# Last chunk of an attention and quantised feed-forward kernel: a tile's residual and butterflies issued ahead of a unit's division, its transposes ahead of the value products

## The chip, the cores and the metric

The kernel runs on one core of one Trainium2 chip. Such a core has five engines with a queue of instructions each: TensorE (PE in the profile; PEld is its loading of weights), VectorE (DVE), ScalarE (ACT), GpSimd (POOL) and SyncE (SP), which here only issues transfers. Each engine takes its own queue strictly in order and waits for others by semaphores. The metric is the time of one execution on the device, in microseconds (us); lower is better.

## The reference

The input x has 8 sequences of 1024 rows of 512 numbers. Cut to what matters:

```python
def attn(x, Wq, bq, Wk, bk, Wv, bv, Wo, bo):          # 16 heads of 32
    Q, K, V = (split_heads(x @ W.T + b) for W, b in ((Wq, bq), (Wk, bk), (Wv, bv)))
    scores = einsum('bhid,bhjd->bhij', Q, K) / sqrt(32)
    delta = t[:, None] - t[None, :]
    scores = where(delta < 0, -inf, scores) - delta   # causal, with a decay by distance
    out = einsum('bhij,bhjd->bhid', softmax(scores), V)
    return join_heads(out) @ Wo.T + bo

def ffn(x, weight):
    xh = x @ H                                        # Hadamard matrix, 512 x 512
    scale = clip(max(abs(xh), axis=-1), 1e-05) / 7
    xq = clip(round(xh / scale), -8, 7) * scale       # 4 bits
    return einsum('bsi,oi->bso', xq, ternary(weight))

x = x + layernorm(attn(layernorm(x), Wq, bq, Wk, bk, Wv, bv, Wo, bo))
x = x + layernorm(ffn(layernorm(x), weight))
```

## The kernel before

Rows are worked on in 16 chunks of 512, two to a sequence; a chunk has four tiles of 128 rows. Since the score falls by one for each row of distance, only a band of keys is used: a block of 128 queries sees its own 128 keys and the 128 before them. (A flag, `ok`, is worked out near the end from the largest products; if it says that the band isn't enough, a general path runs after it. With the inputs here it doesn't.)

**Units.** Attention is done in units: 256 queries (half a chunk) of four heads, so eight units to a chunk, in two halves of four. A unit has four steps. `scores()` puts 48 small products on TensorE (L571) into one PSUM tile `s`, and four exponentials on ScalarE (L585) from `s` into `pr`. `mask()` is one `affine_select` on GpSimd over `pr` (L596). `values()` multiplies `pr` with V (L626) and with ones, for the sums of the softmax (L637), into the PSUM tile `av`. `divide()` is four VectorE instructions (L655, L657, L659, L660) that read `av` and write a part of `oT`, the attention's output transposed. There is one buffer of `av` alone: the `values()` of a unit can start on TensorE only when the `divide()` of the unit before it has read `av` to its end (L660).

**Rests.** What follows attention is done tile by tile by a generator, `rest`; `steps(gen, n)` lets it run over n of its yields. Its steps: load the residual rows `xr` (L182); project with Wo into `o_ps` (L153); `y`, its statistics (L187, L126, L127 on VectorE) and one over the deviation, `rstd_a`, on GpSimd (L119, L120), then `ca` (L191); the residual sum `x1` (L194) and the two butterfly stages of the Hadamard transform, `u` (L198, L199) and `w` (L202, L203), on VectorE; four transposes of `w` into `wT_ps` (L210) and a copy of them to SBUF on ScalarE (L212); the product with the 128x128 Hadamard matrix into `h_ps` (L218) and its sum of squares (L226); the row's largest value `sc` (L238) and the scale (L240 to L243); the quantised row `qf` on ScalarE (L246) and `qi` on VectorE (L248); transposes of `qi` (L255) and their copy (L257); the product with the ternary weights into `f_ps` (L153 again, bf16); `y2` (L264); its statistics, and the last sum and the transfer out (L281 to L286). The last five tiles also have idle products put ahead of some of these, the warm products: L208 ahead of the transposes of `w`, L216 ahead of the Hadamard product, L253 ahead of the transposes of `qi`. Their results are overwritten.

**PSUM banks.** The rests share three banks, and `bank(held)`, `bank(one)`, `bank(two)` name the one that the next tile gets.

**The last chunk.** All order is written out by hand: each engine gets its instructions in the order in which the program issues them. In 15 of the 16 chunks the units are interleaved with the projections of the next chunk. The last chunk has no next one, and its loop (from `for u in range(2, 2 * NG, 2)`) interleaves units with rests alone: two units and one whole rest to a turn. In a turn, `late`, `rest_b` and `rest_a` are three tiles at different steps: `rest_a` is projected (`o_ps`, `y`) in one turn, becomes `rest_b` in the next, and there gets its transposes, its Hadamard product and all up to `y2`; then it is `late`. Before the loop comes a first turn written out by itself, and after it the tail, whose order is a string of letters.

There are four places where a tile's `x1`, butterflies and transposes meet two divisions; this text numbers them by turn. In place 1 the tile is 0_2 (tile 2 of the sequence's first chunk) and the units are 0 and 1 of the last chunk; in place 2 it is tile 0_3 with units 2 and 3; in place 3 tile 1_0 with units 4 and 5; in place 4 tile 1_1 with units 6 and 7, at the start of the tail. The first unit of each pair is called the even one, the second the odd one.

Of the kernel before, what the change touches and what calls it, by code (L numbers as in the profile page):

```python
# [40 lines left out]
def sandwich_kernel(  # L41
# [262 lines left out]
    def band():  # L304
# [212 lines left out]
        def diagonal(col, n):  # L517
            diag = row.tile([P, P], F32, tag="diag", name=f"diag_{n}", bufs=1)
            nc.vector.tensor_scalar(diag, ident, col, None, ALU.mult)
            return diag  # L520

        def spread_max(diag, n):

            ps = pools.ps_m.tile([P, P], F32, tag="pm", name=f"m_ps_{n}")
            nc.tensor.matmul(ps, ones, diag, start=True, stop=True)
            m = small.tile([P, 1], F32, tag="spread", name=f"spread_{n}")
            nc.vector.tensor_reduce(m, ps, AX.X, ALU.max)
            return m
# [263 lines left out]
        def steps(gen, count):  # L792
            for _ in range(count):
                if gen is not None:
                    next(gen)
# [15 lines left out]
        def bank(at):  # L811
            pools.ps_m.named = at
# [3 lines left out]
        held, one, two = 0, 1, 2  # L816
        unit = None
        rest_a = rest_b = None
        for at, ch in enumerate(chunks[:-1]):
# [7 lines left out]
            for u in range(0, 2 * NG, 2):  # L827

                new = Unit(ch, before, u)
# [6 lines left out]
                unit = new  # L836
# [13 lines left out]
                rest_b = rest_a  # L850
# [5 lines left out]
                rest_a = next(rests_due) if at or u >= 4 else None  # L856
# [9 lines left out]
                new = Unit(ch, before, u + 1)  # L866
                new.scores()
                unit.values()
                if u >= 4:
                    held, one, two = one, two, held  # L870
# [21 lines left out]
                unit = new  # L892
                if u == 6:
# [11 lines left out]
                    held, two = two, held  # L905
                else:
# [6 lines left out]
                    held, one, two = one, two, held  # L913
# [9 lines left out]
        new = Unit(ch, before, 0)  # L923
# [3 lines left out]
        unit = new  # L927
        steps(rest_a, 1)
        new = Unit(ch, before, 1)
        new.scores()  # L930
        unit.mask()
        rest_b, rest_a = rest_a, next(rests_due)
# [5 lines left out]
        steps(rest_b, 1)  # L938
        steps(rest_a, 1)
        unit.values()  # L940
        steps(rest_b, 1)
        new.mask()
        unit.divide()
        unit = new
        for u in range(2, 2 * NG, 2):
            late, rest_b, rest_a = rest_b, rest_a, next(rests_due)
            steps(rest_b, 1)
            new = Unit(ch, before, u)
            new.scores()
            unit.values()  # L950
            unit.divide()
            unit = new
            unit.mask()
            bank(held)
            steps(rest_b, 1)
            bank(one)
            steps(rest_b, 2)
            steps(late, 1)
            steps(rest_b, 1)
            new = Unit(ch, before, u + 1)  # L960
            new.scores()
            bank(two)
            steps(rest_a, 1)
            steps(rest_b, 1)
            new.mask()
            steps(late, 1)
            bank(held)
            steps(rest_b, 1)
            unit.values()
            steps(rest_a, 1)  # L970
            unit.divide()
            unit = new
            bank(one)
            steps(rest_b, 2)
            if u == 2:
                diag = diagonal(allmax, "all")
            elif u == 4:
                bank(held)
                okm = spread_max(diag, "all")
                nc.vector.tensor_scalar(ok, okm, (BAND_LIMIT / SLACK) ** 2, None, ALU.is_le)  # L980
            one, two = two, one

        late, rest_b, rest_a = rest_b, rest_a, next(rests_due)
        rest_c = next(rests_due)
        tails = {"l": late, "b": rest_b, "a": rest_a, "c": rest_c}
        steps(rest_b, 1)
        unit.values()
        unit.divide()
        order = "b0 b1 b l b a2 b l b0 a b1 c0 b a c a2 a1 b c a a c0 a c2 c c a0 a1 b c a c0 a c2 c c a c"
        for step in order.split():  # L990
            if step[1:]:
                bank((held, one, two)[int(step[1:])])
# [237 lines left out]
    with tc.manual_schedule():  # L1230
        band()
# [47 lines left out]
```

## Time and profile before

Three runs took 1395.66, 1396.66 and 1398.48 us; the median is 1396.66.

| what | value |
|---|---|
| the profiled execution's own time | 1396.07 us |
| its span, from the first to the last instruction | 1394.3 us |
| mean granted TensorE clock | 0.995 |
| first scores of the last chunk on TensorE | 1295.98 us |
| from there to the end | 98.3 us |
| TensorE busy, 1250 to 1290 us (loop of the other chunks) | 39.91 of 40 us |
| TensorE busy, 1310 to 1350 us (last chunk) | 36.29 of 40 us |
| VectorE busy, 1310 to 1350 us | 28.08 of 40 us |
| GpSimd busy, 1310 to 1350 us | 18.10 of 40 us |

A line of the timeline gives the start and the length of an instruction in us, its engine, its line in the kernel, its operation, the tile that it writes and those that it reads, and in brackets how long its engine was idle before it and whose end released it. A line of the stretches gives start and end, then the busy time of each engine in it with the number of its instructions, then the TensorE clock that was granted as a share of full speed, and the share and rate of the transfers. The page's chain of waits is empty for this run, so that the order of events has to be read from the timelines.

### The profile page before, as it was taken

To read this page: it belongs to the slowest core of one execution; us is meant where nothing else is said; L and a number is where in the kernel's file an instruction comes from. 1 tells how busy PE (TensorE), PEld (TensorE's weight loads), DVE (VectorE), ACT (ScalarE), POOL (GpSimd) and SP (SyncE) were. 2 spreads that over 40 slices of the span, in tenths; PEclk is the share of its full clock that TensorE was granted. 3 is DMA by queue.
4 is the path that set the end of the run, shared out by engine and by line. 5 is a ranking of instruction groups with operands and counts; after the bars stand their busy time and mean duration, and the time that the engine had idled before them with its cause. 6 is when DMAs were issued, how large, how long until landed. Compare 5 with 4: busy or idle time off the path is not lost.

```text
span 1394.3 us, 35003 instructions
## 1 busy us (share of the span) xinstructions
PE 1363.4 (98%) x14504; PEld 967.5 (69%) x14504; DVE 1015.7 (73%) x2167; ACT 681.2 (49%) x1176; POOL 892.0 (64%) x1280
## 2 busy tenths in 40 slices
PE   9999999999999999999999999999999999999895
PEld 5577777777767777767776777777776777766553
DVE  5467777777777776777777777877777777777675
ACT  3345454545445455554545545445544545535442
POOL 4565758576576767658676676757757666665434
PEclk9999999999999999999999999999999999999998
DMA  6010011011011011011011011011101101000010
GB/s 228 8 47 24 24 47 46 24 47 47 24 47 47 24 47 47 32 39 47 30 41 46 25 47 47 28 43 47 40 31 47 47 24 47 25 23 32 32 39 33
DMA packets 31750, 58.23 MB, mean 42 GB/s; under 512 B 4064, under 2 KB 4448, under 8 KB 31584
## 3 DMA queue, kind: packets, MB, share of 16 engines
q1 hardware_dynamic: 30720, 54.87, 11.4%
q8 instruction: 116, 1.90, 0.5%
q10 hardware_dynamic: 864, 1.05, 0.2%
q14 instruction: 50, 0.41, 0.1%
HBM read 39.13 MB, written 16.78 MB: 40 GB/s over the span
## 4 chain that ended last, share of the span: by engine, by line


## 5 line engine op out<-in xcount | busy, mean ns | idle before, releaser
L585 ACT ACTIVATE pr<-s,bias 128x512 f32<-128x512 f32 (+1 forms) x512 | 295.3, 660 | 138.5 <-PE s L571 138.5
L610 POOL TENSOR_TENSOR both<-pr 128x1024 f32<-128x1024 f32 (+1 forms) x120 | 250.5, 2088 | 5.2
L153 PE MATMUL o_ps<-wo_sb,oT 128*128 128x512 f32 x512 | 236.1, 604 | 0.6
L596 POOL TENSOR_SCALAR_AFFINE_SELECT pr<-pr 128x1024 f32<-128x1024 f32 x128 | 150.0, 1172 | 108.2 <-ACT pr L585 103.8
L153 PEld LDWEIGHTS o_ps<-wo_sb,oT 128*128 128x128 f32 x512 | 93.2, 192 | 95.2 <-issue 92.5
L187 DVE TENSOR_TENSOR y<-o_ps,bo 128x512 f32<-128x512 f32 x64 | 44.2, 691 | 150.5 <-PE o_ps L153 150.5
L626 PE MATMUL av<-pr,v 128*32 128x128 f32 (+1 forms) x2816 | 130.7, 316 | 1.8 <-DVE oT L660 1.8
L571 PE MATMUL s<-qT,kT 32*64 32x192 f32 (+2 forms) x5632 | 119.9, 285 | 1.5 <-ACT pr L585 1.5
L571 PEld LDWEIGHTS s<-qT,kT 32*64 32x64 f32 x5632 | 99.8, 131 | 31.0 <-issue 21.6
L141 ACT ACTIVATE xn<-xc,nmr,rstd_n 128x512 f32<-128x512 f32 x60 | 48.8, 814 | 140.0 <-POOL nmr L139 140.0
L119 POOL TENSOR_SCALAR rstd_a<-mv_a 128x1 f32<-128x1 f32 x64 | 13.9, 217 | 142.7 <-DVE mv_a L127 141.5
L226 ACT ACTIVATE wT<-h_ps 128x512 f32<-128x512 f32 x64 | 38.2, 597 | 133.8 <-PE h_ps L218 133.8
L626 PEld LDWEIGHTS av<-pr,v 128*32 128x32 f32 x2816 | 74.9, 110 | 35.4 <-issue 1.8
L212 ACT COPY wT<-wT_ps 128x512 f32<-128x512 f32 x64 | 37.5, 585 | 123.4 <-PE wT_ps L210 123.4
L238 DVE TENSOR_REDUCE sc<-h_ps 128x1 f32<-128x512 f32 x64 | 44.1, 689 | 63.8 <-ACT wT L226 63.8
L119 POOL TENSOR_SCALAR rstd_c<-mv_c 128x1 f32<-128x1 f32 x64 | 14.7, 229 | 116.1 <-DVE mv_c L127 116.0
L285 POOL TENSOR_TENSOR y<-y,x 128x512 f32<-128x512 f32 x63 | 80.6, 1279 | 1.3 <-ACT y L284 1.3
L637 PE MATMUL av<-both,ones 128*32 128x256 f32 x960 | 74.2, 381 | 0.5 <-POOL both L614 0.5
L218 PEld LDWEIGHTS h_ps<-had_sb,wT 128*128 128x128 f32 x512 | 66.8, 192 | 6.2 <-ACT wT L212 3.3
L218 PE MATMUL h_ps<-had_sb,wT 128*128 128x128 f32 x512 | 68.1, 276 | 2.1 <-ACT wT L212 2.1
L153 PE MATMUL f_ps<-ternT,qiT 128*128 128x512 bf16 x256 | 66.2, 382 | 2.4 <-ACT qiT L257 2.4
L146 ACT COPY xnT<-xnT_ps 128x512 f32<-128x512 f32 x60 | 35.2, 586 | 56.8 <-PE xnT_ps L145 56.8
(213 smaller groups left out, 3100.7 us busy)
## 6 DMA issues: line engine op xcount, KB each, us to landing
xr<-in_x SPq DMA_DIRECT2D x64, 256.0 KB, 2.9
out<-y SPq DMA_DIRECT2D x63, 256.0 KB, 2.0
xc<-in_x SPq DMA_DIRECT2D x60, 256.0 KB, 2.7
wv_sb<-in_wvT ACTq DMA_DIRECT2D x4, 256.0 KB, 5.1
x<-in_x SPq DMA_DIRECT2D x4, 256.0 KB, 4.9
wk_sb<-in_wkT SPq DMA_DIRECT2D x1, 1024.0 KB, 6.7
wq_sb<-in_wqT SPq DMA_DIRECT2D x1, 1024.0 KB, 9.0
wf_sb<-in_wf SPq DMA_DIRECT2D x1, 1024.0 KB, 10.7
```

The source lines that it names most:

```text
L141: nc.scalar.activation(xn, xc, AF.Identity, bias=nmr, scale=r)
L153: nc.tensor.matmul(ps, lhs(k), rhs(k), start=(k == 0), stop=(k == KD - 1))
L187: nc.vector.tensor_tensor(y, ps, bo2, ALU.add)
L218: nc.tensor.matmul(xh[:, k * P : (k + 1) * P], wT[:, k, :], had_sb if k else had0_sb, start=True, stop=True,)
L238: nc.vector.tensor_reduce(sc, xh, AX.X, ALU.max, apply_absolute_value=True)
L285: nc.gpsimd.tensor_tensor(y2, y2, x1, ALU.add)
L571: nc.tensor.matmul(s[half * hp : (half + 1) * hp, hh, column[which] + c0 : column[which] + c1], kc.kT[hsl, g, k0 : k0 + hp], ch.qT[hsl, g, ...
L585: nc.scalar.activation(pr[:, :, r0:, own, cols], s5[:, :, r0:, own, cols], AF.Exp, bias=ch.bias[:, own, h : h + 1],)
L596: nc.gpsimd.affine_select(out=own, in_=own, compare_op=ALU.is_ge, fill=0.0, base=0, pattern=[[0, HPG], [0, 2], [1, P]], channel_multiplier=-1,
L610: engine.tensor_tensor(self.both[:, :, r0:], pr[:, :, r0:, 0, :], pr[:, :, r0:, 1, :], ALU.add)
L626: nc.tensor.matmul(av[hh * HD : (hh + 1) * HD, 0, qc : qc + w], kc.v[:, at, h * HD : (h + 1) * HD], pr[:, hh, sc : sc + w], start=(at_part ...
L637: nc.tensor.matmul(av[hh * HD : (hh + 1) * HD, 1, :], ones[:, :HD], self.both[:, hh].rearrange("p r c -> p (r c)") if own is None else sel ...
```

## The change

Four things are moved in the last chunk, and nothing is added or taken away.

- In the first turn and in each turn of the loop the step that holds a tile's `x1` and butterflies (L194 to L203) is issued ahead of the division of the even unit, where it was issued behind it. In the first turn the `y2` of the tile before (L264) moves behind the division too.
- The step that holds the transposes of `w` with their warm products and the copy (L208, L210, L212) is issued ahead of the value products of the odd unit, where it was behind them and behind their division.
- The product that spreads the largest value for the flag (L525, in the turn u = 4) gets the bank `two` in place of `held`.
- At the tail the transposes are issued ahead of the value products of the last unit, and the string of the tail begins one step later.

On the queues this gives: TensorE has L208 and L210 of the four tiles ahead of the odd unit's L626 and L637; VectorE has L194 to L203 of the four tiles ahead of the even unit's L655 to L660; ScalarE and GpSimd have the same order as before; on SyncE the load of `xr` for tile 1_2 stands ahead of the read of the flag, where it stood behind it.

```diff
         steps(rest_b, 1)
         steps(rest_a, 1)
         unit.values()
+        new.mask()
+        steps(rest_a, 1)
+        unit.divide()
         steps(rest_b, 1)
-        new.mask()
-        unit.divide()
         unit = new
         for u in range(2, 2 * NG, 2):
             late, rest_b, rest_a = rest_b, rest_a, next(rests_due)
-            steps(rest_b, 1)
             new = Unit(ch, before, u)
             new.scores()
+            bank(held)
+            steps(rest_b, 1)
             unit.values()
             unit.divide()
             unit = new
             unit.mask()
-            bank(held)
-            steps(rest_b, 1)
             bank(one)
             steps(rest_b, 2)
...
             bank(held)
             steps(rest_b, 1)
             unit.values()
-            steps(rest_a, 1)
+            steps(rest_a, 2)
             unit.divide()
             unit = new
             bank(one)
...
             elif u == 4:
-                bank(held)
+                bank(two)
                 okm = spread_max(diag, "all")
...
         tails = {"l": late, "b": rest_b, "a": rest_a, "c": rest_c}
+        bank(held)
         steps(rest_b, 1)
         unit.values()
         unit.divide()
-        order = "b0 b1 b l b a2 b l b0 a b1 c0 b a c a2 a1 b c a a c0 a c2 c c a0 a1 b c a c0 a c2 c c a c"
+        order = "b1 b l b a2 b l b0 a b1 c0 b a c a2 a1 b c a a c0 a c2 c c a0 a1 b c a c0 a c2 c c a c"
```

## The prediction

> **What bounds the kernel now.** I read the busy shares first, then TensorE's waits between 1308 and 1362 us (the chain of waits is empty), then the last chunk's timelines, engine by engine.
>
> ```profile
> PE 1363.4 (98%) x14504; PEld 967.5 (69%) x14504; DVE 1015.7 (73%) x2167; ACT 681.2 (49%) x1176; POOL 892.0 (64%) x1280
> ```
>
> TensorE is nearly always busy, but the change touches only the last chunk, where it waits (total us, times, longest):
>
> ```profile
> PE qiT_ps L255 <- DVE qi L248: 2.3, 3, 0.8
> PE av L626 <- DVE oT L660: 1.8, 2, 0.9
> PE h_ps L218 <- ACT wT L212: 1.5, 4, 0.7
> ```
>
> The third wait is for the copy of the transposes, which the change puts beside the value products. The second is the odd unit's value products waiting for the even unit's division, and that division the change delays. Place 2, TensorE, then VectorE with GpSimd's `rstd_a`:
>
> ```profile
> 1324.55 0.99 PE L571 MATMUL s<-qT,kT 32*64 32x192 f32 x48
> 1325.49 1.08 PE L626 MATMUL av<-pr,v 128*32 128x256 f32 x24
> ...
> 1327.36 1.09 PE L208 MATMUL wT_ps<-ident 128*128 128x128 f32 x8
> 1328.29 0.76 PE L210 MATMUL wT_ps<-ident,w 128*128 128x128 f32 x4
> ...
> 1329.78 1.16 PE L218 MATMUL h_ps<-had_sb,wT 128*128 128x128 f32 x8 [0.28 <-ACT wT L212]
> ```
>
> ```profile
> 1322.69 0.18 DVE L127 BATCH_NORM_AGGREGATE mv_a<-st_a 128x2 f32<-128x6 f32 x1
> 1323.72 0.45 DVE L655 STREAM_TRANSPOSE sumT<-av 128x256 f32<-128x256 f32 x1 [0.85 <-PE av L637]
> ...
> 1324.92 0.42 DVE L660 TENSOR_TENSOR oT<-av,rn 128x256 f32<-128x256 f32 x1
> ...
> 1326.11 0.75 DVE L194 SCALAR_TENSOR_TENSOR x<-y,rstd_a,xr 128x512 f32<-128x512 f32 x1
> ...
> 1328.37 0.44 DVE L655 STREAM_TRANSPOSE sumT<-av 128x256 f32<-128x256 f32 x1
> ...
> 1323.27 0.57 POOL L120 TENSOR_TENSOR rstd_a<-rstd_a,neghalf 128x1 f32<-128x1 f32 x1
> ```
>
> The reader is to see that the even division ends at 1325.34, just ahead of the value products at 1325.49: it costs TensorE nothing here, with no room left. The whole place hangs on one loop: `qi` of a tile, `y` and statistics of the next, division, odd value products, Hadamard product `h_ps`, next `qi`.
>
> **The change part by part.** I time a place from the end of `qi` (Q) to the start of L218, and keep what follows L218 as it is: from there to the next Q it was 6.42 us at place 2 (1329.78 to 1336.21) as at place 1 (1314.90 to 1321.32), set by ScalarE's squares, the odd exponentials and `qf`, none of which change order.
>
> *Places 2 to 4, new sum.* Statistics end at Q+1.55 (1322.87 against Q = 1321.32), `rstd_a` at Q+2.52 (1323.84). `x1` now starts there, 0.03 later, Q+2.55 (that step after L120 is 0.03 at 1373.40 to 1373.43). From the start of `x1` to the start of the transposing L655 behind it are 2.26 (1326.11 to 1328.37): the division starts at Q+4.81, lasts 1.62 (1323.72 to 1325.34) and ends at Q+6.43. TensorE takes a released value product 0.15 later (oT ends 1355.32, L626 at 1355.47): Q+6.58. Value products and sums take 1.87 (1325.49 to 1327.36): Q+8.45. Two warm products L216 behind them, four records, take half of the eight L208 records' 0.93 (1327.36 to 1328.29), 0.46: L218 at Q+8.91. The transposes themselves cost nothing: scores end at Q+4.17, eight warm records fill to Q+5.10, `w` is ready near Q+5.03, they end by Q+5.7, the copy on ScalarE follows the even exponentials at Q+6.69 and ends at Q+7.3. The value products from Q+6.58 to Q+8.45 hide it; without that cover it would cost the old 0.28.
>
> L218 was at Q+8.46 in place 2, at Q+8.66 in place 3 (1336.21 to 1344.87; it holds L525, 0.31, which now falls into the wait) and at Q+8.30 in place 4 (1351.30 to 1359.60). So: **+0.45, +0.25, +0.61**. Bounds: 0.15 more each if the warm products take the 0.61 of their record; 0.6 less each (then -0.2 at place 2) if they vanish beside the wait (0.46) and `x1` with its butterflies takes its bare steps, 0.75 + 4 x 0.34 = 2.11 in place of 2.26. I take the middle, since TensorE showed that spacing of warm records and VectorE these 2.26 in place 3 too (1341.19 to 1343.45).
>
> *Place 1.* There GpSimd's mask of the odd unit (L596) stands right behind `rstd_a` and `ca`, where VectorE now begins `x1`. What then happens the loop of earlier chunks shows:
>
> ```profile
> 123.37 0.43 DVE L198 TENSOR_TENSOR u<-x 128x256 f32<-128x256 f32 x1
> 123.38 1.38 POOL L596 TENSOR_SCALAR_AFFINE_SELECT pr<-pr 128x1024 f32<-128x1024 f32 x1 [1.67 <-ACT pr L585]
> 123.71 1.33 DVE L199 TENSOR_TENSOR u<-x 128x256 f32<-128x256 f32 x1
> ```
>
> One butterfly takes 1.33 in place of 0.42: +0.91. `rstd_a` ends at 1309.59, `x1` starts at 1309.62, `ca` meets it (0.81, as at 1368.19) and ends about 1310.50, the mask then takes its turn behind L198 and holds L199. The division starts at 1309.62 + 2.26 + 0.91 = 1312.79, ends 1314.41; value products at 1314.56 where they were at 1311.52; 1.87 later, without warm products for this tile, L218 at 1316.43, where it was at 1314.90: **+1.53** (+0.62 if the mask slips by).
>
> *Tail.* `o_ps` of tile 1_2 waits for the last division: 0.13 behind the sums (1353.56 to 1353.69), 1.62, 0.15, so 1.90 after them, where L218's group ends 1.45 after them (0.46 + 0.99). These 0.45 fall into TensorE's wait of 0.54 before L255 at 1364.95: 0; with that cover gone, 0.45.
>
> *The rest of the diff.* The late `y2` of place 1 and L525 in bank `two`: L527 reads it about one us after the division, the next writer there is L216, two us after it: 0. The `xr` load ahead of the flag's read on SyncE is wanted a turn of 15 us later and lands in 2.9: 0. GpSimd and ScalarE keep their order; queued behind the waiting value products are L216, L218 and the odd scores, which is the loss already counted.
>
> *Clock.* Sum so far: 1.53 + 0.45 + 0.25 + 0.61 = **+2.84**. But place 1 now leaves TensorE nearly empty: from 1310.53 to about 1313.0 for `w`, about 0.6 of transposes, and until 1314.56 for the division, 3.4 of 4.0 us. The slow time of the trace lasts 3.41 us, so here are stretches of that length:
>
> ```profile
> 1298.35:1301.76 3.41, 1.45 (x57) 1.25 (x54) 2.67 (x8) 2.99 (x6) 2.20 (x2) 1.00 0.40 114
> 1301.76:1305.17 3.41, 3.41 (x6) 1.33 (x5) 0.00 (x0) 2.07 (x4) 0.00 (x0) 0.50 0.12 45
> ...
> 1363.20:1366.61 3.41, 1.91 (x13) 0.87 (x12) 2.28 (x6) 2.06 (x3) 2.21 (x5) 1.00 0.02 5
> 1366.61:1370.02 3.41, 3.41 (x11) 1.66 (x10) 2.56 (x5) 0.00 (x0) 2.13 (x4) 1.00 0.20 77
> ```
>
> After a stretch with TensorE busy 1.45 the clock (first number behind the counts) is 0.50 for one stretch, after 1.91 it stays 1.00. Place 1 will have a stretch busy for well under 1.7 wherever such stretches begin. A slow one costs at most 1.65: the eight `o_ps` records at 1301.60 took 5.35, at 1331.79 3.70. Part of it falls on the waiting itself; between 0 and 1.65 I take 1.2, nearer the row with full work, since value products, L218 and scores fill it.
>
> [...]
>
> Total **+4.04**. The profiled execution is 1394.3 of span and 1.8 around it, 1396.07, and 0.6 below the median: 1396.07 + 4.04 = **1400.1 us**.
>
> **The rivals.** *Stalls without the clock* (22 of 100): +2.84, or +1.93 without the clash with the mask: 1398.0 to 1398.9. For it: where the 3.41 us stretches begin differs from run to run. Against it: 3.4 of 4 us empty.
>
> *A stretch that no longer falls badly* (11): the run before lost 1.65 to the slow clock at 1301.76, before any moved instruction; if the new run begins its stretches elsewhere, +2.84 − 1.65 gives 1397.3. The 2.8 us between the three runs speak for such play.
>
> *Clock lost at place 4 as well* (10): pauses of about 0.8 and 1.0 there; +1.2 more, 1401.3.
>
> *The other side, faster* (7): the transposes fill the pauses and the division doesn't hold TensorE. Then the old pauses go: 0.92 + 0.87 for `oT`, 0.67 + 3 x 0.28 for the copy, 3.3 in all: 1392.8. It decides by one thing, whether the division ends before the transposes do (Q+5.7); by the rows it ends at Q+6.43, and only a `rstd_a` 0.7 us earlier, with GpSimd as it is, would turn it. That the change doesn't do what it says I don't expect: the queues show it.
>
> **How the numbers follow.** Forecast 50, the others 22, 11, 10, 7. The forecast's own range is 1398.9 (clock at 0) to 1401.5 (clock at 1.65, warm products at their longest, the tail's 0.45). With eight in ten wanted, I go down past the second and third cases to 1397.0 and up to 1402.4. A measurement of this kernel tells about 0.2%, 2.8 us. Over 1399.45: 0.46 of the forecast's 0.50, the place 4 case and 0.08 of the second, 0.64; below 1393.9 the last case, 0.07; within, the rest, 0.29.
>
> **What would show it.** Right: in places 2 to 4, L194 starting where L655 stood, a pause of about 0.9 before the odd L626 put down to oT, none before L218, Q to Q growing to 15.3 us; in place 1 a butterfly of 1.3 us, L626 3 us after the old distance from the scores' start, a slow stretch behind it. Wrong: L626 following L210 with no pause, turns shorter than 14.9 us, or a late L218 that the tail makes good.

## The result, and the profile after

| | before | changed |
|---|---|---|
| median (11 runs each) | 1397.08 us | 1400.77 us |
| lowest to highest | 1394.46 to 1398.77 | 1398.60 to 1402.78 |
| profiled execution, and its span | 1396.07, 1394.3 | 1402.69, 1401.0 |

The changed kernel takes 1.0026 times as long, with a 95% interval of 1.0017 to 1.0035: +3.6 us (2.4 to 4.9). The chain of waits is empty again. TensorE's waits between 1308 and 1366 us of the changed kernel (total us, times, longest):

```profile
PE av L626 <- DVE oT L660: 3.7, 4, 1.1
PE wT_ps L210 <- DVE w L202: 2.5, 2, 2.1
PE qiT_ps L255 <- DVE qi L248: 2.4, 3, 0.8
```

The wait for the copy of the transposes (1.5 us before) is gone. The wait of the odd value products for the even division has come at all four places, where it was at two, and at two places there is a wait for `w` that was not there. Place 2, TensorE's timeline, then VectorE's:

```profile
1327.82 0.99 PE L571 MATMUL s<-qT,kT 32*64 32x192 f32 x48
1328.74 1.09 PE L208 MATMUL wT_ps<-ident 128*128 128x128 f32 x8
1329.67 0.60 PE L210 MATMUL wT_ps<-ident,w 128*128 128x128 f32 x4
1331.16 1.08 PE L626 MATMUL av<-pr,v 128*32 128x256 f32 x24 [0.90 <-DVE oT L660]
1332.03 1.07 PE L637 MATMUL av<-pr,ones 128*32 128x256 f32 x16
1333.03 0.71 PE L216 MATMUL h_ps<-ones 128*128 128x128 f32 x4
1333.58 1.06 PE L218 MATMUL h_ps<-had_sb,wT 128*128 128x128 f32 x8
```

```profile
1323.47 1.12 DVE L248 TENSOR_SCALAR qi<-qf 128x512 bf16<-128x512 f32 x1 [1.28 <-ACT qf L246]
...
1327.14 0.75 DVE L194 SCALAR_TENSOR_TENSOR x<-y,rstd_a,xr 128x512 f32<-128x512 f32 x1 [1.00 <-POOL rstd_a L120]
...
1329.40 0.44 DVE L655 STREAM_TRANSPOSE sumT<-av 128x256 f32<-128x256 f32 x1
...
1330.59 0.42 DVE L660 TENSOR_TENSOR oT<-av,rn 128x256 f32<-128x256 f32 x1
```

`x1` now begins 1.00 us after VectorE fell idle, released by GpSimd. The division starts 2.26 behind it, and TensorE, done with its transposes, stands for 0.90 until the division's last instruction lets `av` go. Place 1, VectorE and then GpSimd:

```profile
1309.96 0.75 DVE L194 SCALAR_TENSOR_TENSOR x<-y,rstd_a,xr 128x512 f32<-128x512 f32 x1 [1.00 <-POOL rstd_a L120]
1310.75 0.42 DVE L198 TENSOR_TENSOR u<-x 128x256 f32<-128x256 f32 x1
1311.09 1.33 DVE L199 TENSOR_TENSOR u<-x 128x256 f32<-128x256 f32 x1
...
1310.80 1.34 POOL L596 TENSOR_SCALAR_AFFINE_SELECT pr<-pr 128x1024 f32<-128x1024 f32 x1
```

and what TensorE makes of it:

```profile
1313.03 0.79 PE L210 MATMUL wT_ps<-ident,w 128*128 128x128 f32 x4 [2.09 <-DVE w L202]
1314.89 1.93 PE L626 MATMUL av<-pr,v 128*32 128x256 f32 x24 [1.08 <-DVE oT L660]
1316.57 1.65 PE L637 MATMUL av<-pr,ones 128*32 128x256 f32 x16
```

The value products take 1.93 and 1.65 us in place of 1.08 and 1.07. The stretches say why (columns as before; the first number behind the last bracket is TensorE's clock):

```profile
1310.97:1314.39 3.42, 0.79 (x4) 0.45 (x4) 3.28 (x8) 2.96 (x5) 2.03 (x2) 1.00 0.25 79
1314.39:1317.80 3.41, 2.91 (x36) 1.98 (x40) 1.01 (x2) 0.05 (x1) 0.25 (x1) 0.50 0.02 5
1317.80:1321.21 3.41, 3.41 (x67) 2.39 (x60) 2.60 (x6) 1.55 (x4) 0.74 (x2) 1.00 0.00 0
1358.77:1362.18 3.41, 1.89 (x18) 1.19 (x20) 3.27 (x9) 0.59 (x1) 0.00 (x0) 1.00 0.24 77
1362.18:1365.59 3.41, 3.41 (x42) 2.15 (x32) 0.51 (x2) 0.00 (x0) 0.00 (x0) 0.50 0.01 2
```

Half clock follows place 1's empty stretch and, in this execution, place 4's too. The two profiled spans differ by 6.70 us, more than the medians. By distances between instructions this splits as follows. The last chunk's first scores come 2.03 later (1298.01 against 1295.98), through code that is the same. `o_ps` of the first turn takes 3.65 in place of 5.35: -1.70. From the even scores (place 1) or the end of `qi` (places 2 to 4) to the Hadamard product L218: +2.92, +0.53, +0.33, +2.33. From L218 to the next `qi`: -0.17 in all. From the last of these L218 to the end: +0.43. So the four places cost 5.9 us in this execution, 3.0 of it clock.

### The profile page after: what moved, and what is told of

Same layout as the page of the kernel before. It is cut to its first block, busy times and chain, and to the rows that moved or that the text cites. A ratio compares the mean times of both kernels' runs of the same rounds, so it can differ in the third digit from the quotient of the medians.

```text
span 1401.0 us, 34943 instructions
## 1 busy us (share of the span) xinstructions
PE 1362.8 (97%) x14441; PEld 967.9 (69%) x14504; DVE 1018.1 (73%) x2167; ACT 681.7 (49%) x1176; POOL 896.0 (64%) x1280
## 4 chain that ended last, share of the span: by engine, by line
## 5 line engine op out<-in xcount | busy, mean ns | idle before, releaser
L626 PE MATMUL av<-pr,v 128*32 128x128 f32 (+1 forms) x2816 | 132.2, 318 | 3.7 <-DVE oT L660 3.7
L626 PEld LDWEIGHTS av<-pr,v 128*32 128x32 f32 x2816 | 75.4, 110 | 38.0 <-issue 4.1
L212 ACT COPY wT<-wT_ps 128x512 f32<-128x512 f32 x64 | 37.6, 587 | 118.6 <-PE wT_ps L210 118.6
L637 PE MATMUL av<-both,ones 128*32 128x256 f32 x960 | 74.2, 381 | 0.5 <-POOL both L614 0.5
L218 PEld LDWEIGHTS h_ps<-had_sb,wT 128*128 128x128 f32 x512 | 66.7, 191 | 4.5 <-ACT wT L212 0.9
L153 PE MATMUL f_ps<-ternT,qiT 128*128 128x512 bf16 x193 | 63.0, 384 | 5.9 <-ACT qiT L257 2.6
L218 PE MATMUL h_ps<-had_sb,wT 128*128 128x128 f32 x512 | 67.8, 275 | 0.6 <-ACT wT L212 0.6
L655 DVE STREAM_TRANSPOSE sumT<-av 128x256 f32<-128x256 f32 x128 | 55.7, 435 | 12.0 <-PE av L637 11.4
```

The lines of the kernel that those rows point to most:

```text
L153: nc.tensor.matmul(ps, lhs(k), rhs(k), start=(k == 0), stop=(k == KD - 1))
L218: nc.tensor.matmul(xh[:, k * P : (k + 1) * P], wT[:, k, :], had_sb if k else had0_sb, start=True, stop=True,)
L626: nc.tensor.matmul(av[hh * HD : (hh + 1) * HD, 0, qc : qc + w], kc.v[:, at, h * HD : (h + 1) * HD], pr[:, hh, sc : sc + w], start=(at_part ...
L637: nc.tensor.matmul(av[hh * HD : (hh + 1) * HD, 1, :], ones[:, :HD], self.both[:, hh].rearrange("p r c -> p (r c)") if own is None else sel ...
L655: nc.vector.transpose(st.rearrange("p b c -> p (b c)"), av[:, 1, :])
```

## The experiments

Twelve runs followed, eleven kernels and the changed one again, all timed in turn with the kernel before on their chip; that median moved between 1394.84 and 1396.08 us from set to set, so ratios count, not times. (The ratios are not simply the quotients of the two medians.) Since a ratio's interval is 1.2 to 2.0 us to either side, the distances in the profiles, one profile for each kernel, carry most of the weight. They are, in us:

| kernel | place 1, even scores to L218 | place 2, qi to L218 | place 3 | place 4 |
|---|---|---|---|---|
| before | 5.29 | 8.46 | 8.66 | 8.30 |
| changed | 8.21 | 8.99 | 8.99 | 10.63 |
| changed, run again | 8.52 | 8.98 | 8.98 | 8.98 |
| VectorE part alone | 9.28 | 12.17 | 10.70 | 10.69 |
| transposes alone | 7.49 | 11.71 | 10.27 | 11.50 |
| mask ahead of `rstd_a` | 5.91 | 8.99 | 8.98 | 10.61 |
| pauses filled | 6.81 | 8.99 | 8.98 | 9.04 |
| neither clash nor pauses | 5.91 | 8.98 | 8.99 | 9.04 |

**The two halves alone.** First VectorE's half: transposes back behind the value products.

```diff
             new.scores()
-            bank(held)
-            steps(rest_b, 1)
             unit.values()
             unit.divide()
             unit = new
             unit.mask()
+            bank(held)
+            steps(rest_b, 1)
```

(and the same at the tail).

> The VectorE part of the change alone: residual and butterflies ahead of the even division, transposes back behind the odd unit's value products. Theory (the late division is the loss, the transposes ahead of the value products give some of it back): the odd value products again start 6.57 us after qi at places 2 to 4, as in the changed kernel, but the Hadamard product now comes 4.1 to 4.3 us behind their start (value products, warm products, transposes, copy) in place of 2.4: 10.7 to 10.9 us after qi, against 8.3 to 8.7 before and 8.99 in the changed kernel. Over four places +10 us against before, and up to 4 more where TensorE's pause of 2.4 us ahead of the value products halves the clock: 1407 to 1411 us. Rival (the transposes ahead of the value products are the loss, the order on VectorE costs nothing): the Hadamard product at its old 8.3 to 8.7 us after qi, about 1397 us.

Measured: 1409.24 us, ratio 1.0104 (1.0089 to 1.0118), 14.5 us. Place 3, where the clock stayed full, from TensorE's timeline of this kernel:

```profile
1348.69 0.99 PE L571 MATMUL s<-qT,kT 32*64 32x192 f32 x48
1351.82 1.08 PE L626 MATMUL av<-pr,v 128*32 128x256 f32 x24 [2.13 <-DVE oT L660]
...
1355.95 1.16 PE L218 MATMUL h_ps<-had_sb,wT 128*128 128x128 f32 x8 [0.28 <-ACT wT L212]
```

With no transposes to do, TensorE stands for the division 2.13 us, does the value products, and only then the transposes: L218 4.13 behind L626. `qi` ended at 1345.25, so L626 is at 6.57, as in the changed kernel. The rival, that VectorE's order is free, falls. Then TensorE's half, on the kernel before:

```diff
             new.scores()
+            bank(held)
+            steps(rest_b, 1)
             unit.values()
             unit.divide()
             unit = new
             unit.mask()
-            bank(held)
-            steps(rest_b, 1)
```

> The TensorE part of the change alone: transposes ahead of the odd unit's value products, VectorE's order as before (division, then the late y2, then residual and butterflies). Theory: w is ready 6.9 to 7.3 us after qi as before, TensorE now stands at the transposes until then with the value products behind them, and the Hadamard product comes about 10.0 us after qi, 1.6 later than before at each of places 2 to 4 and about 1.3 later at place 1: +6.2 us, and up to 4 more from a halved clock behind pauses of 2.1 us: 1403 to 1407 us. Rival (only VectorE's order costs, TensorE's order is free): as before, about 1397 us. With the run of the VectorE part alone: both halves alone slower than both together would show that neither half is the loss by itself, but what it makes wait.

Measured: 1406.23 us, ratio 1.0082 (1.0069 to 1.0095), 11.4 us. Its place 3:

```profile
1345.63 1.09 PE L208 MATMUL wT_ps<-ident 128*128 128x128 f32 x8 [0.49 <-DVE spread_all L527]
1347.75 0.88 PE L210 MATMUL wT_ps<-ident,w 128*128 128x128 f32 x4 [1.03 <-DVE w L202]
1348.57 1.07 PE L626 MATMUL av<-pr,v 128*32 128x256 f32 x24
```

Now `w` is late, and the value products, long free to go, stand behind the transposes in TensorE's queue. Both losses lie a little above what was expected against before; in both profiles the clock was halved at two or more places (the sums at places 1 and 2 took 1.75 and 1.74 us in the first, 1.95 each in the second, in place of 1.07). Each half alone costs three to four times what both cost together, so neither is the loss by itself. The VectorE half makes `w` early and `oT` late, the TensorE half puts `w`'s consumer first, and together one wait for `oT` is left (at places 1 and 4 also one for `w`, 2.09 and 0.44 us).

**The clash with the mask.**

```diff
         steps(rest_b, 1)
+        new.mask()
         steps(rest_a, 1)
         unit.values()
-        new.mask()
         steps(rest_a, 1)
         unit.divide()
```

> The changed kernel with the odd unit's mask of the first turn issued ahead of the projection's statistics, so that GpSimd does it in its idle time and not beside the butterflies. Theory (the mask holds one butterfly for 0.91 us): all four butterflies of place 1 at 0.42 us, the odd value products 4.04 us after the start of the even scores in place of 4.95; -0.9 us, and a further 0 to -1.4 where the shorter pause spares the clock: about 1399.4 us, against 1400.8. Rival (the butterfly of 1.33 us has another cause, or the value products wait for something else): no change at place 1, 1400.8 us.

Measured: 1399.09 us, ratio 1.0025 (1.0014 to 1.0035). VectorE and GpSimd at place 1 of this kernel:

```profile
1311.14 0.42 DVE L199 TENSOR_TENSOR u<-x 128x256 f32<-128x256 f32 x1
...
1303.84 1.10 POOL L596 TENSOR_SCALAR_AFFINE_SELECT pr<-pr 128x1024 f32<-128x1024 f32 x1 [2.40 <-ACT pr L585]
```

With the mask done 7 us earlier the butterfly is back to 0.42 from 1.33, and the value products come 4.04 us after the even scores in place of 4.95: the 0.91 is the mask's. The time doesn't show it: the ratio is no clear step under the changed kernel's. In the profiled execution the clock was spared at place 1 and halved at place 4 (sums of 1.07 and 2.00 us). How the mask holds the butterfly no run shows.

**The pauses.** Idle products, whose results nothing reads, in TensorE's pauses.

```diff
-        WARM = {..., 3: (8, 2, 4), 4: (8, 2, 0), 5: (8, 2, 0)}
+        WARM = {..., 3: (11, 2, 4), 4: (8, 2, 0), 5: (8, 2, 0), 6: (16, 0, 0)}
+        def fill(count):
+            bank(one)
+            pt = pools.ps_m.tile([P, KD, P], F32, tag="pm", name=f"fill_{count}")
+            for _ in range(count):
+                nc.tensor.transpose(pt[:, 0, :], ident, ident)
...
             bank(held)
             steps(rest_b, 1)
+            if u == 2:
+                fill(10)
             unit.values()
...
         bank(held)
         steps(rest_b, 1)
+        fill(11)
         unit.values()
```

> The changed kernel with TensorE's pauses of places 1 and 4 filled by idle products: 16 ahead of place 1's transposes and 10 behind them, 3 more ahead of place 4's and 11 behind. Nothing waits for them but the products behind them, and they fit the pauses. Theory (the pauses halve the clock for one stretch): value products and sums of places 1 and 4 take 1.87 us in every profile in place of 3.3, no clock under full speed from 1310 us to the tail, and the start of the value products stays at 4.95 us after the even scores and 6.57 us after qi; the median comes down by 1.2 to 2.2 us to about 1399.0, with less spread between runs. Rival (the clock's drop costs nothing in the end, or comes from something else): value products at 3.3 us or 1.87 as before, median 1400.8 us or, if the idle products are in the way, above.

Measured: 1398.56 us, ratio 1.0023 (1.0013 to 1.0033). Place 1 on TensorE:

```profile
1312.52 0.88 PE L210 MATMUL wT_ps<-ident,w 128*128 128x128 f32 x4
1313.24 1.25 PE L927 MATMUL fill<-ident 128*128 128x128 f32 x10
1314.48 1.08 PE L626 MATMUL av<-pr,v 128*32 128x256 f32 x24
1315.35 1.07 PE L637 MATMUL av<-pr,ones 128*32 128x256 f32 x16
```

The value products start no sooner (4.94 us after the even scores) and are at full speed, at place 4 too. The profile of the next kernel, with its pauses filled as well, shows the same, and over all runs the mean granted clock is 0.9951 for the changed kernel (23 runs) and 0.9964 for these two (20 runs). So in these runs the slow clock came from the pauses. The runs lie closer (1396.94 to 1400.10), but the median's gain over the changed kernel, expected at 1.2 to 2.2, is inside the intervals.

**Both together, the changed kernel again, and the kernel before with its pauses filled.** The first has the mask moved as above, 8 idle products ahead of place 1's transposes and the rest of the fillings as above.

> The changed kernel with the mask of the first turn ahead of the statistics and with TensorE's pauses of places 1 and 4 filled (8 and 10 idle products at place 1, 3 more and 11 at place 4). What is left of the change is the order on VectorE and TensorE alone. Theory (late division +0.6, +0.45, +0.25, +0.6 at the four places; the mask +0.9; the clock the rest): odd value products at 4.04 us after the even scores at place 1 and 6.57 after qi at the others, value products and sums 1.87 us everywhere; +1.9 us against before, ratio 1.0014, 2.0 under the changed kernel. Rival (the mask or the clock carry all of the loss): ratio 1.000.

> The changed kernel itself once more, on the chip of these runs, so that the edits on it can be set against it directly. Both theories: ratio 1.0026 as measured first, between 1.002 and 1.0035; in its profile place 1 with value products 4.95 us after the even scores and place 1, or 1 and 4, at half clock.

Measured: 1396.56 us, ratio 1.0004 (0.9995 to 1.0012), and 1399.33 us, ratio 1.0028 (1.0018 to 1.0037), in one set. Clash and clock are most of the loss: without them 2.8 us of it are gone, and the order alone costs 0.6 (-0.7 to +1.7). How the 2.8 us divide between the two the times don't show: singly, the two edits had brought the ratio only from 1.0026 to 1.0025 and 1.0023, inside the intervals. By its distances the order should cost 1.93 (+0.62, +0.52, +0.33, +0.74, less 0.28 between L218 and `qi`), just outside that interval. But how large this gap is depends on how the runs are summed up: the plain medians of the set differ by 1.72 us, the means by 1.08. One more kernel asked whether the kernel before loses to the clock as well. The edit puts 11 idle products behind the last value products of the chunk before, 6 ahead of the odd ones at places 1 and 4, and 4 ahead of place 1's L218.

> The kernel before, its order untouched, with idle products in its own pauses of the last chunk: 11 behind the last value products of the chunk before, 6 ahead of the odd value products of place 1 and 6 at place 4, 4 ahead of place 1's Hadamard product. It asks why the changed kernel without clash and pauses came out at 1.0004 where the distances in its profile give +1.95 us (1.0014). If the kernel before loses to the clock too, in some of its runs, as its first profile shows at o_ps (5.35 us for 3.70), filling its pauses takes 0.5 to 1.2 us off its median, ratio 0.9993, and its slowest runs go. If not, ratio 1.0000, the places at 8.46, 8.66 and 8.30 us after qi, and the gap stays open, within the spread of the runs.

Measured: 1395.49 us, ratio 0.9999 (0.9990 to 1.0008). `o_ps` was at 3.65, but there is no gain: the gap, 1.3 us by the ratio and 0.2 by the medians, is not explained by this and stays open.

In the run again the slow clock at place 1 lasted two stretches, 1311.19 to 1318.02 us, and the loss reached the Hadamard product itself, which took 1.95 us in place of 1.16: L218 started 1.70 later than the sum without clock (8.52 against 6.82), and from L218 to `qi` it was 7.22 in place of 6.42.

**What the change wanted, had otherwise.** If an early `w` is worth having, two other things on the kernel before stand in its way. GpSimd's mask holds `qi` (1.12 us in place of 0.43), and the late `y2` stands on VectorE ahead of `x1`. First the mask, moved behind `ca`:

```diff
             steps(rest_b, 1)
-            new.mask()
             steps(late, 1)
             bank(held)
             steps(rest_b, 1)
             unit.values()
             steps(rest_a, 1)
+            new.mask()
             unit.divide()
```

> The kernel before, with the odd unit's mask in the three turns of the loop issued on GpSimd behind rstd_a and ca of the next projection, not beside qi. Theory (GpSimd's mask holds the quantising qi, 1.12 us in place of 0.43, and qi ends the wait of TensorE at L255): qi at 0.43 us, TensorE's pause of 0.78 ahead of L255 down to about 0.1, each turn 0.5 to 0.7 us shorter (qi to qi 14.3 in place of 14.9), the odd value products still not waiting for the mask: -1.5 to -2.1 us against before, ratio 0.9987. Rival (the mask comes too late for the odd value products now, or holds another VectorE instruction): a new pause of 0.5 us or more at L626 or a butterfly of 1.3, and no gain.

Measured: 1393.86 us, ratio 0.9983 (0.9974 to 0.9992), 2.4 us under before. VectorE's `qi` and GpSimd's mask:

```profile
1319.48 0.43 DVE L248 TENSOR_SCALAR qi<-qf 128x512 bf16<-128x512 f32 x1 [1.28 <-ACT qf L246]
...
1322.84 1.11 POOL L596 TENSOR_SCALAR_AFFINE_SELECT pr<-pr 128x1024 f32<-128x1024 f32 x1
```

From L218 to the end of `qi` it is 5.73 in place of 6.43, three times 0.70. One part of the expectation failed without cost: at place 4 the profile puts the wait of the odd value products (0.87 us) down to the mask now and no longer to `oT`, but they start 4.17 us after `qi` as before. Next the late `y2` (L264), with the flag's instructions, behind the butterflies:

```diff
-        WARM = {..., 3: (8, 2, 4), 4: (8, 2, 0), 5: (8, 2, 0)}
+        WARM = {..., 3: (4, 2, 4), 4: (4, 2, 0), 5: (4, 2, 0)}
...
             steps(rest_b, 1)
+            if u > 2:
+                steps(late, 1)
             new = Unit(ch, before, u)
...
             bank(one)
-            steps(rest_b, 2)
+            steps(rest_b, 1)
...
```

The rest of the edit moves the flag's instructions behind the next even division (L525 in the turn u = 6, in bank `two`) and gives the tail the same order. The warm products ahead of the transposes go from eight to four in the same edit, and so in all kernels below; this was not tried apart. By the rows of place 2 (4.17 + 1.87 + 0.93) eight of them would have held TensorE until 6.97 us after `qi`, so an earlier `w` alone would have gained little.

> The kernel before, with the late tile's y2 (and the flag's instructions) behind the next tile's residual and butterflies in place of ahead of them; the division stays ahead of both; warm products ahead of the transposes 4 in place of 8. Theory (what the change wanted, w earlier, is to be had without delaying the division): w ends 6.35 us after qi in place of 6.93 to 7.33, the odd value products stay at 4.17, the Hadamard product comes 7.7 us after qi in place of 8.3 to 8.7 at places 2 to 4: -2.0 to -2.6 us, ratio 0.9984. Rival (w isn't what the Hadamard product waits for, but the copy behind the exponentials or TensorE's own queue): Hadamard product at 8.3 or later, no gain.

Measured: 1394.43 us, ratio 0.9990 (0.9981 to 0.9999). L218 came 7.85 us after `qi` at places 2 and 4, but 9.08 at place 3; of the 2.0 to 2.6 us expected, 1.4 came (0.1 to 2.7). Both edits together:

> Both of the last two edits on the kernel before. Theory (the two cut different parts of the turn, qi's and w's): qi to qi about 13.5 us in place of 14.9, -3.5 to -4.7 us against before, ratio 0.997. Rival (they hide the same wait): no better than the better of the two, ratio 0.9985.

Measured: 1393.27 us, ratio 0.9973 (0.9962 to 0.9984). Its TensorE waits name the culprit at place 3:

```profile
PE m_ps_all L525 <- DVE y L264: 0.9, 1, 0.9
```

The flag's product had been put into the bank that the `y2` reads, which the same edit had made later. Idle products in the first turn of this kernel gave nothing:

> The same with idle products in TensorE's pauses of the first turn: 11 behind the last value products of the chunk before, 6 ahead of the odd value products of place 1, and 4 ahead of its Hadamard product. Theory (a stretch of 3.41 us in which TensorE is busy for less than about half halves the clock for the next one): the projection o_ps of the first turn always at 3.7 us, where it was 5.35 in the profile before; 0 to -0.8 us at the median against the run of both edits, ratio 0.9965, and a smaller spread. Rival (the idle products get in the way): first turn longer by 0.1 to 0.5 us and no gain.

Measured: 1393.43 us, ratio 0.9975 (0.9965 to 0.9985). Last, the flag's product moved into the tail, behind the last of the four L218:

```diff
-            elif u == 6:
-                bank(two)
-                okm = spread_max(diag, "all")
...
-        order = "b0 b1 b l b a2 ..."
+        order = "b0 b1 m2 b l b a2 ..."
         for step in order.split():
             if step[1:]:
                 bank((held, one, two)[int(step[1:])])
+            if step[0] == "m":
+                okm = spread_max(diag, "all")
...
+                continue
```

> Both edits (mask clear of qi, late y2 behind the butterflies), with the flag's product moved into the tail: in the earlier run of both it stood in bank two ahead of place 3's transposes and waited 0.88 us for the y2 that the edit had put later. Theory: place 3's Hadamard product 7.85 us after qi, as at places 2 and 4, where it was 9.07; -1.2 us against the run of both edits, -4.0 to -4.9 against before, ratio 0.9967. Rival (the flag's product costs as much wherever it stands): as the run of both, 0.9973.

Measured: 1390.50 us, ratio 0.9962 (0.9949 to 0.9975), the fastest here: 5.3 us under before (3.5 to 7.1). L218 is at 7.85 at places 2, 3 and 4, and TensorE's own queue nearly closes:

```profile
1326.86 1.16 PE L218 MATMUL h_ps<-had_sb,wT 128*128 128x128 f32 x8 [0.28 <-ACT wT L212]
1327.95 0.99 PE L571 MATMUL s<-qT,kT 32*64 32x192 f32 x48
1328.87 3.70 PE L153 MATMUL o_ps<-wo_sb,oT 128*128 128x512 f32 x8
1332.66 0.40 PE L255 MATMUL qiT_ps<-ident_bf,qi 128*128 128x128 bf16 x4
```

The pause of 0.78 ahead of L255 is gone. It gets `w` earlier by moving the late `y2`, for which nobody waits at these places once the flag's product is out of the way, where the change moved the division, for which TensorE waits.

## Why the prediction was right

The forecast case came: 1400.77 us against 1400.1, +3.6 against +4.04, with the division as the cause.

*Places 2 to 4.* The odd value products were forecast 6.58 us after `qi`; they came at 6.57 three times. L218 was forecast at 8.91 and came at 8.99, since two warm products take 0.55 between L637 and L218 and not 0.46. The 0.08 came back behind it: L218 no longer waits for the copy and passes on after 0.99 us in place of 1.09, which the prediction, keeping all behind L218 as it was, had not seen. Net +0.44 and +0.23 at places 2 and 3 against +0.45 and +0.25; at place 4, in the run again, where its clock stayed full, +0.68 up to L218 against +0.61. The transposes cost nothing, as said.

*Place 1.* The clash was forecast by analogy with the earlier chunks, and came as there: L199 at 1.33, `ca` at 0.82, value products 4.95 us after the even scores (1314.56 less 1309.61 in the sum), and the run with the mask moved shows the mask to be its cause.

*Clock.* Forecast at 1.2 for place 1, bounded by 1.65. The first profile gives 1.39 on value products and sums; the run again lost 1.70 up to L218 and 0.80 behind it, above the bound, because the slow clock lasted two stretches there. So both profiles lie above the 1.2, and the range of this term was too narrow. The place 4 case, given 10 in 100, showed in the first profile and in that with the mask moved, not in the run again: as far as three profiles can say, it was priced too low.

*Tail.* Taken as 0. In the run again it is 34.46 from place 4's L218 to the end, 34.70 before: 0 holds. The reading behind it doesn't: `o_ps` was to stand 0.45 for the last division, but it started right behind L218 (1364.04 in the run again), 0.31 before that division ended, and took its usual 3.60.

*The sum.* The order alone, +1.93 by its terms, has +1.93 by the distances and 0.6 (-0.7 to 1.7) by the measured times; with the clash, the terms give +2.84. So the terms are shown by the distances of each place, but the total only within its interval of 2.4 to 4.9. That it came so near +4.04 is in part luck: in the first profile the clock cost 3.0 us where 1.2 was forecast, and `o_ps`, ahead of the moved instructions, gave 1.70 back.

*The rivals.* The run with the pauses filled is the second case, made on purpose. The third, a lucky `o_ps`, happened in the first profile (3.65), and was outweighed. The faster case falls with the two halves alone: the late division does hold TensorE.

## What to carry to other kernels

An instruction may be moved ahead on its engine only past work for which nobody on the path waits: look for whom the passed one releases, with its buffers, not only for what the moved one gains. Where two moves depend on each other, try each alone: here both halves were worse than the whole. And a pause on TensorE may have to be priced twice, for itself and for the clock behind it: in the first profile of the changed kernel place 1 had pauses of 2.09 and 1.08 us, and at a clock of 0.50 the value products and sums behind them took 1.39 us more.

## What the runs showed of the hardware

In these profiles the half clock keeps a beat. Before, it starts at 1301.76 and 1383.68, 81.92 us apart, 24 times 3.413; in the changed kernel's at 1314.39 and 1362.18, 47.79 apart, 14 times 3.414. Among the products of the last chunk it lasts one or two beats of 3.41; the one that starts at 1383.68 lasts to the end of the execution, where TensorE has almost nothing left to do. So here the same pauses were punished or spared by where the beat fell: place 4 has the same pauses (0.43 and 1.08 us) in the run again, but there the beat parts them, TensorE is busy 2.34 us in the one that holds the longer, and the next one is at full clock. In a beat TensorE was busy 0.79, 1.45 and 1.59 us ahead of slow ones, and 1.91 ahead of a full one; but 1.89 ahead of a slow one as well (place 4 above), and in the run of the VectorE part alone, with the beat laid by its slow products, 1.47 and 1.52 ahead of full ones, so busy time by the profile, with its modelled ends, doesn't give the line sharply. The 1.7 of the prediction and the "less than about half" of an expectation were estimates from the rows with 1.45 and 1.91.

Short pauses were enough here. In the profile before, pauses of 1.49 and 0.47 us with 0.99 of scores between them stand ahead of the slow stretch at 1301.76; in the changed kernel's, 2.09 and 1.08 with 0.79 of work between them at place 1, and 0.44 and 1.08 at place 4, stand ahead of those at 1314.39 and 1362.18.
